# Float32r score passes on exact halves of q and k, a mask done by ScalarE and GpSimd, shared buffer pools and re-measured planner durations

## The chip, the cores and the metric

The kernel runs on one core of one Trainium2 chip. The time is the device time in microseconds of one execution; lower is better. The kernel before was timed three times: 977.66, 982.55 and 979.96 us, median 979.96 us. One execution was profiled; it took 974.69 us, of which the profile's span (first to last instruction) is 972.9 us.

The core has five engines: TensorE (PE in the profile, its weight loads PEld), VectorE (DVE), ScalarE (ACT), GpSimd (POOL) and SyncE (SP, here only a queue that issues DMAs). Each runs its own instruction list in order and waits on semaphores of the others.

## What is computed

One Macaron transformer block in float32 on x of shape (4, 1024, 256): four sequences of 1024 tokens.

```
x = x + 0.5 * ffn(layernorm(x))
x = x + attention(layernorm(x))
x = x + 0.5 * ffn(layernorm(x))

ffn(x):        hdn = silu(x @ gate_w.T * gate_s) * (x @ up_w.T * up_s)      # 704 wide, ternary weights
               out = hdn @ down_w.T * down_s
attention(x):  q, k, v = x @ Wq.T, x @ Wk.T, x @ Wv.T                       # 16 heads of 16
               q, k = rope(q), rope(k)
               out = softmax(causal(q @ k.T / 4)) @ v;  out @ Wo.T
```

## The kernel before

Tokens are worked on in 8 blocks of 512 (two blocks for each sequence). For each block there are a first FFN (`ffn(i, 1)`), `qkv(i)`, the attention, and a second FFN (`ffn(i, 2)`). The causal mask makes the second block of a sequence look at twice the keys of the first.

*FFN.* Activations and weights are in float32r, a type that TensorE multiplies in one pass where float32 takes more. An activation is kept as two float32r tiles, its rounded value and the rest (`xh` and `xnT`, `hh` and `hl`), so each product is two matmuls: L717 (gate and up, 128x512) and L804 (down, 128x256). ACT does tanh, scaling and rounding, DVE and POOL the multiplications and subtractions.

*Attention.* A group g holds 4 heads, each on 32 partitions, so that four small matmuls can stand side by side in the array ("32*128" in the profile is a matmul on 32 rows). In `qT` a head's 32 rows are 16 of q and 16 of k; DMAs (`split`, L971) copy k into the tile `kT`, whose other rows are zero but the last, which holds ones. The scores are computed twice:

- `max_half` (L1045): queries on partitions, for the maximum of each row. DVE adds the causal mask to the diagonal parts in PSUM (L1070) and takes the negated maximum (`reduce`, L1097 and L1080).
- `row_of_max` (L1119 to L1133) turns these maxima with a matmul and sends them by DMA into the last row of each head in `qT`. That row has been cleared by a DMA before (`clear`, L994).
- `exp_half` (L1158): keys on partitions. The last rows (ones against maxima) subtract the maximum within the matmul. ACT takes exp into `pT` (L1167), POOL zeroes what is masked (L1179), and `weigh` multiplies with v (L1205).

Score matmuls are float32. A "half" is two heads (a `pair`) of one unit of up to 512 columns; two halves of different pairs make a burst, so all four row groups of the array are in use. Each half takes two PSUM banks of the eight.

*The order of the work.* Nothing is ordered at run time: the class `Planner` is run while the program is built. It is a list scheduler: every operation has an engine (or a choice of DVE and POOL, `either`), a duration in us, a `tail` (time until its result can be used), the buffers it takes and a priority; bursts of scores are put in at intervals (`GAP`) between the dense matmuls. The instruction lists of all engines, and of the SP queue, come out of this plan. Each kind of tile has buffers of its own (`shapes`); `todo` is the order in which FFNs are begun. The planner's formulas for durations are `mm_us`, `dve_us` and `act_us`.

The program holds a second copy in plain float32 behind a test on the ternary weights; it is not executed here.

## Time and profile before

| what | before |
|---|---|
| three timed runs, median | 979.96 us |
| the profiled execution | 974.69 us, span 972.9 us |
| PE busy | 919.1 us (94%) |
| DVE busy | 810.8 us (83%) |
| ACT busy | 560.9 us (58%) |
| POOL busy | 542.0 us (56%) |
| granted TensorE clock, mean | 0.975 |
| DMA | 46.48 MB |

"Busy" is the union of an engine's instructions. A busy PE is not a PE at its peak, because matmuls overlap and their ends are modelled; the time from one matmul's start to the next says more. The chain of waits follows the work that ended last backwards, from each instruction to what released it. In the lists of groups, a line gives engine, operation, out<-in, shapes, count, then the busy time, the mean duration of one in ns, and the idle time of the engine before them with what ended it.

### The profile page before, as it was taken

The numbers are of one execution on the slowest core, as the hardware profiler recorded it, in microseconds if no ns is written. First come the engines' busy times: TensorE is split into PE (matmuls) and PEld (weight loads), VectorE is DVE, ScalarE is ACT, GpSimd is POOL, SyncE is SP. The second block draws the span as 40 slices with busy tenths as digits, with TensorE's granted clock in tenths as the row PEclk, the third lists the DMA queues.
The fourth block names the chain that finished last, engine by engine and source line by source line (L and its number), as shares of the span: only waits on it lengthen the run. The fifth ranks groups of instructions, "written<-read, shape, count | busy, mean of one in ns | idle before, by whom it ended". The sixth has DMA issues, their size and how long they took to land.

```text
span 972.9 us, 20459 instructions
## 1 busy us (share of the span) xinstructions
PE 919.1 (94%) x7672; PEld 525.0 (54%) x7672; DVE 810.8 (83%) x1842; ACT 560.9 (58%) x1048; POOL 542.0 (56%) x691
## 2 busy tenths in 40 slices
PE   7599998999999999998999999999999999999996
PEld 6456653465654545455556545465555453445565
DVE  5789977999798979986899978878979798997375
ACT  4554682257774555384857548268565553667663
POOL 5236785774773255755747468458652566656320
PEclk8799999999999999999999999999999998999998
DMA  8130103421302002211100302100300021020000
GB/s 295 47 85 3 44 3 76 123 66 44 88 1 88 3 14 57 67 45 39 51 1 2 110 14 77 40 8 18 92 9 16 14 73 36 26 56 7 23 23 26
DMA packets 42596, 46.48 MB, mean 48 GB/s; under 512 B 5164, under 2 KB 29996, under 8 KB 42476
## 3 DMA queue, kind: packets, MB, share of 16 engines
q1 hardware_dynamic: 41752, 44.55, 16.1%
q8 instruction: 63, 1.03, 0.4%
q10 hardware_dynamic: 736, 0.53, 0.2%
q14 instruction: 45, 0.37, 0.1%
HBM read 25.40 MB, written 15.20 MB: 42 GB/s over the span
## 4 chain that ended last, share of the span: by engine, by line
PE 66%; DVE 20%; ACT 4%; POOL 4%; issue 3%; DMA 2%; SPq 1%; ACTq 0%; DVEq 0%; POOLq 0%
PE bank L1045 14%; PE bank L717 13%; PE bank L1158 13%; PE bank L1205 11%; PE bank L804 8%; PE bank L574 7%; DVE nm L1097 5%; DVE bank L1070 2%; DVE ta L747 2%; ACT pT L1167 1%; DVE st L521 1%; DMA xnT<-xd 1%; DVE st L538 1%; DVE ta L753 1%; POOL hl L760 1%
## 5 line engine op out<-in xcount | busy, mean ns | idle before, releaser
L1167 ACT ACTIVATE pT<-bank 128x512 f32<-128x512 f32 x576 | 300.4, 602 | 186.5 <-PE bank L1158 184.3
L1097 DVE TENSOR_REDUCE nm<-bank 128x1 f32<-128x512 f32 (+2 forms) x640 | 330.8, 573 | 10.4 <-PE bank L1158 9.1
L1158 PE MATMUL bank<-qT,kT 32*128 32x512 f32 (+3 forms) x1536 | 315.8, 519 | 4.8 <-DVE ta L747 1.5
L1045 PE MATMUL bank<-kT,qT 32*128 32x512 f32 (+3 forms) x1536 | 295.9, 509 | 0.2 <-ACT tb L750 0.2
L1045 PEld LDWEIGHTS bank<-kT,qT 32*128 32x128 f32 x1536 | 128.8, 186 | 79.7 <-issue 32.8
L1158 PEld LDWEIGHTS bank<-qT,kT 32*128 32x128 f32 x1536 | 132.9, 185 | 45.8 <-issue 11.0
L1179 POOL TENSOR_SCALAR_AFFINE_SELECT pT<-pT 128x256 f32<-128x256 f32 x256 | 100.2, 413 | 96.4 <-ACT pT L1167 95.7
L717 PE MATMUL bank<-xh,wgu_sb 128*128 128x512 f32 (+1 forms) x354 | 149.9, 424 | 2.9 <-ACT xh L689 2.2
L717 PE MATMUL bank<-xnT,wgu_sb 128*128 128x512 f32 (+1 forms) x354 | 143.4, 405 | 1.5 <-POOL xnT L692 1.1
L1205 PE MATMUL bank<-pT,va 128*32 128x512 f32 (+3 forms) x1536 | 137.1, 489 | 0.8 <-ACT pT L1167 0.5
L1070 DVE TENSOR_TENSOR bank<-bank,causal 128x256 f32<-128x256 f32 (+1 forms) x320 | 103.8, 370 | 12.0 <-PE bank L1158 11.2
L753 POOL TENSOR_TENSOR ta<-ta,tb 128x512 f32<-128x512 f32 (+1 forms) x70 | 89.4, 1282 | 43.0 <-DVE ta L747 23.5
L804 PE MATMUL bank<-wd_sb,hl 128*128 128x256 f32 x320 | 87.8, 300 | 10.1 <-POOL hl L760 5.1
L717 PEld LDWEIGHTS bank<-xh,wgu_sb 128*128 128x128 f32 x354 | 68.2, 193 | 51.6 <-ACT pT L1167 20.7
L747 DVE SCALAR_TENSOR_TENSOR ta<-ta,bank 128x512 f32<-128x512 f32 (+1 forms) x96 | 64.8, 679 | 37.0 <-ACT ta L744 25.2
L760 POOL TENSOR_TENSOR hl<-ta,hh 128x512 fp32r<-128x512 f32 x63 | 81.4, 1298 | 21.3 <-ACT hh L756 19.4
L804 PE MATMUL bank<-wd_sb,hh 128*128 128x256 f32 x320 | 89.1, 305 | 4.2 <-ACT hh L756 4.2
L1205 PEld LDWEIGHTS bank<-pT,va 128*32 128x32 f32 x1536 | 44.9, 109 | 88.4 <-issue 50.0
L744 ACT ACTIVATE ta<-bank,gus_sb 128x512 f32<-128x512 f32 (+1 forms) x96 | 66.3, 691 | 35.7 <-PE bank L717 32.6
L717 PEld LDWEIGHTS bank<-xnT,wgu_sb 128*128 128x128 f32 x354 | 68.2, 193 | 17.0 <-POOL xnT L692 2.0
L804 PEld LDWEIGHTS bank<-wd_sb,hh 128*128 128x128 f32 x320 | 64.2, 201 | 22.8 <-issue 16.3
L804 PEld LDWEIGHTS bank<-wd_sb,hl 128*128 128x128 f32 x320 | 64.2, 201 | 14.1 <-POOL hl L760 7.2
(93 smaller groups left out, 1124.8 us busy)
## 6 DMA issues: line engine op xcount, KB each, us to landing
xd<-xs SPq DMA_DIRECT2D x84, 128.0 KB
xnT<-xd SPq DMA_DIRECT2D x21, 512.0 KB
rp<-in_rope SPq DMA_DIRECT2D x8, 512.0 KB
kT<-qT SPq DMA_DIRECT2D x64, 64.0 KB
out<-x SPq DMA_DIRECT2D x16, 256.0 KB
x<-in_x SPq DMA_DIRECT2D x7, 512.0 KB
qT<-nmT SPq DMA_DIRECT2D x128, 2.0 KB
tb<-in_wgu SPq DMA_DIRECT2D x5, 256.0 KB
```

Of the source, the lines that this page charges most:

```text
L717: nc.tensor.matmul(d.tile[:, j * P : (j + n) * P], wgu_sb[:, k, cols], view(t.tile[:, k])[:, j : j + n], start=k == m == 0, stop=k == NC - ...
L747: nc.vector.scalar_tensor_tensor(a.tile[up], a.tile[gate], 1.0, d.tile[gate], ALU.add, ALU.mult)
L753: e.tensor_tensor(a.tile[up], a.tile[up], u.tile[up], ALU.mult)
L760: e.tensor_tensor(hl[c].tile, a.tile, raw(hh[c].tile), ALU.subtract)
L804: nc.tensor.matmul(d.tile[:, ts(m, D)], t.tile[:, ts(j + m, P)], wd_sb[:, c, :], start=n == k == 0, stop=n == NI - 1 and k == len(halves(c ...
L1045: nc.tensor.matmul(sc[e].tile[:, c0 : c0 + w], qT[blk].tile[r, g, ts(j, P)], kt.tile[r, g, :w], start=True, stop=True,)
L1070: nc.vector.tensor_tensor(d, d, causal.unsqueeze(1).to_broadcast([P, len(masked), P]), ALU.add)
L1097: nc.vector.tensor_reduce(nm.tile[:, o : o + 1], sc[e].tile[:, c0 : c0 + w], AX.X, ALU.max, negate=True)
L1158: nc.tensor.matmul(sc[e].tile[:, c0 : c0 + w], kt.tile[r, g, ts(k % NB, P)], qT[blk].tile[r, g, BLK - w :], start=True, stop=True,)
L1167: nc.scalar.activation(pT.tile[:, e, :w], sc[e].tile[:, :w], AF.Exp)
L1179: nc.gpsimd.affine_select(out=d, in_=d, compare_op=ALU.is_ge, fill=0.0, base=0, pattern=[[0, 2], [1, P]], channel_multiplier=-1,)
L1205: nc.tensor.matmul(av.tile[ts(r, HP), BLK - w :], va[base + k // NB].tile[:, k % NB, h * VS : h * VS + HP], pTs[u, r // 2].tile[:, r % 2, ...
```

## The change

Scores (`max_half`, `exp_half`). After rope, q and k are rounded to float32r by ACT (`high`, tile `qh`) and the rest is taken by POOL or DVE (`low`, tile `ql`). DMAs build three stacks for each head's 32 rows (`moves`): `kh` holds the high half of k over its low half; `qh` holds the high half of q twice; `ql` its low half twice. One matmul of `qh` with `kh` gives (high of q) times (both halves of k), one of `ql` with `kh` the rest: two float32r passes in place of a float32 matmul. In `exp_half` a third pass, `ones` against the tile `mx`, subtracts the maximum, which itself is held in two halves. The 64 moves of k, the 16 clears and 3 loads of ones become 256 moves; the 128 sends of maxima stay, and carry two rows each.

Maxima. DVE no longer adds the mask in PSUM. It reduces the columns off the diagonal straight from PSUM; ACT copies the diagonal parts to a tile `dg` (`copy`), POOL masks them there (`affine_select`), and DVE reduces them from there. `row_of_max` joins the parts and splits the result in two halves (`halves`).

Buffers. Most SBUF kinds now share two pools, `large` (31 buffers) and `small` (22).

Planner. Tails by engine (`TAIL`), shorter durations for several operations, other costs for changes of the array's mode, bursts that emit the passes of both halves interleaved, an earlier burst where no dense matmul is at hand (`EAGER`). FFNs begin in the order of `ORDER`. Block 1's first FFN is transposed by matmuls instead of through DRAM (`TURNED`).

```diff
+ORDER = "10 11 12 13 20 14 21 15 22 16 17 23 24 25 26 27"
+PACE = 0.0
+LEAD = 20.0
+TURNED = ((0, 1), (1, 1), (7, 2))
+TAIL = dict(pe=0.25, dve=0.1, act=0.15, pool=0.1, dma=2.0)
...
+    EAGER = 0.3
-    CHANGE = dict(full=0.2, row=0.2, col=0.12)
+    CHANGE = dict(full=0.25, row=0.25, col=0.15)
...
+            if dense is None or dense > max(b[0], pe) + self.EAGER:
+                at = max(b[0], pe)
...
+                parts = []
+                for h in b[1]:
+                    t = max(at, self.pairs[h.pair])
+                    self.pairs[h.pair] = t + h.us + more
+                    parts += [(t + n * h.us / len(h.parts), f) for n, f in enumerate(h.parts)]
...
+def half_us(passes, cols):
+    return passes * cols / 2400
+
 def dve_us(n):
-    return n / 960 + 0.07
+    return n / 960 + 0.065
 def act_us(n, ptr=0):
-    return n / 1200 + 0.09 + 0.09 * ptr
+    return n / 1200 + 0.055 + 0.09 * ptr
...
+    slots = dict(large=(31, [P, 2 * BLK]), small=(22, [P, BLK]), tiny=(6, [P, D]), bank=(8, [P, BLK]))
+    shared = dict(
+        **dict.fromkeys(("x", "qh", "ql", "kh", "pT", "xnT", "xh", "xs", "rp"), "large"),
+        **dict.fromkeys(("qc", "qs", "ta", "tb", "hh", "hl", "hL", "oq", "on", "dg", "aT"), "small"),
...
-        by_dma = (i, which) not in ((0, 1), (NBLK - 1, 2))
+        by_dma = (i, which) not in TURNED
...
             def both(e=nc.gpsimd):
-                e.tensor_tensor(qT[blk].tile[:, g, :], qc.tile, qs.tile, ALU.add)
+                e.tensor_tensor(qs.tile, qc.tile, qs.tile, ALU.add)
+            def high():
+                nc.scalar.copy(qh[blk][n].tile[:, a, :], qs.tile)
+            def low(e=nc.gpsimd):
+                e.tensor_tensor(
+                    ql[blk][n].tile[:, a, :], qs.tile, qh[blk][n].tile[:, a, :].bitcast(F32), ALU.subtract
+                )
...
-        def split(gs):
+        def moves(n, which):
             def emit():
+                q, l, k = (t[blk][n].tile.bitcast(F32) for t in (qh, ql, kh))
                 for h in range(GH):
-                    nc.sync.dma_start(
-                        out=kT[blk].tile[h * HP : h * HP + HD, gs], in_=qT[blk].tile[h * HP + HD : (h + 1) * HP, gs]
-                    )
+                    lo, hi = slice(h * HP, h * HP + HD), slice(h * HP + HD, (h + 1) * HP)
+                    for to, of in ((q[hi], q[lo]), (l[hi], l[lo])) if which else ((k[lo], q[hi]), (k[hi], l[hi])):
+                        nc.sync.dma_start(out=to, in_=of)
...
+            first = Op("dma", 4.8, moves(n, 0), need, [kh[blk][n]], own, tail=2.2, prio=0)
+            T_done[1, blk, n] = Op("dma", 4.8, moves(n, 1), [first], uses=own, tail=2.2, prio=0)
...
 # max_half
+        def emit(item):
+            (g, j, _, c0, w, _), kt, n = item
+            qt = (qh, ql)[n][blk][g // 2].tile
+            for e in range(2):
+                r = ts(2 * pair + e, HP)
+                nc.tensor.matmul(
+                    sc[e].tile[:, c0 : c0 + w],
+                    qt[r, g % 2, ts(j, P)],
+                    kt.tile[r, g % 2, :w],
+                    start=n == 0,
+                    stop=n == 1,
+                )
...
-                    nc.vector.tensor_tensor(d, d, causal.unsqueeze(1).to_broadcast([P, len(masked), P]), ALU.add)
...
+                    c0, w = u[3], u[4] - P * u[5]
...
+                    nc.scalar.copy(dg.tile[:, e, : len(diag), :], of[:, diag[0] : diag[-1] + 1 : step, :])
...
+                    nc.gpsimd.affine_select(
+                        out=d,
+                        in_=d,
+                        compare_op=ALU.is_ge,
+                        fill=MASKED,
...
+                nc.vector.tensor_reduce(to, of, AX.X, ALU.max, negate=True)
...
 # row_of_max
+            nc.vector.tensor_reduce(all_, parts[:, :, 1 - blk % BPS :], AX.X, ALU.min)
...
+            nc.vector.tensor_copy(hi.bitcast(F32R), all_)
+            nc.vector.tensor_tensor(lo, all_, hi, ALU.subtract)
...
 # exp_half
+        def emit(item):
+            (g, k, c0, w), qt, n = item
+            kt = kh[base + k // NB][g // 2].tile
+            for e in range(2):
+                r = ts(2 * pair + e, HP)
+                if n < 2:
+                    key, query = kt[r, g % 2, ts(k % NB, P)], qt.tile[r, g % 2, BLK - w :]
+                else:
+                    key, query = ones[r, :], qt.tile[r, BLK - w :]
+                nc.tensor.matmul(sc[e].tile[:, c0 : c0 + w], key, query, start=n == 0, stop=n == 2)
```

## The prediction

> **What bounds the kernel now.** I read the page first: busy times, then the chain of waits; then the groups of instructions with shapes kept apart; then stretches of the timeline for what one matmul costs.
>
> ```profile
> PE 919.1 (94%) x7672; PEld 525.0 (54%) x7672; DVE 810.8 (83%) x1842; ACT 560.9 (58%) x1048; POOL 542.0 (56%) x691
> PE 66%; DVE 20%; ACT 4%; POOL 4%; issue 3%; DMA 2%; SPq 1%; ACTq 0%; DVEq 0%; POOLq 0%
> PE bank L1045 14%; PE bank L717 13%; PE bank L1158 13%; PE bank L1205 11%; PE bank L804 8%; PE bank L574 7%; DVE nm L1097 5%; DVE bank L1070 2%; DVE ta L747 2%; ACT pT L1167 1%; DVE st L521 1%; DMA xnT<-xd 1%; DVE st L538 1%; DVE ta L753 1%; POOL hl L760 1%
> ```
>
> PE is the bound, DVE close behind. The two score stages (L1045, L1158) are 27% of the span on the chain; DVE's maxima and mask (L1097, L1070) are 7%. ACT and POOL are busy nearly as long as each other and hardly on the chain. Next, starts of neighbouring matmuls in the timeline.
>
> ```profile
> 300.33 0.28 PE L804 MATMUL bank<-wd_sb,hh 128*128 128x256 f32 x1
> 300.45 0.28 PE L804 MATMUL bank<-wd_sb,hl 128*128 128x256 f32 x1
> 305.33 0.59 PE L1045 MATMUL bank<-kT,qT 32*128 32x512 f32 x2
> 305.77 0.59 PE L1045 MATMUL bank<-kT,qT 32*128 32x512 f32 x2
> 306.20 0.59 PE L1045 MATMUL bank<-kT,qT 32*128 32x512 f32 x2
> 400.26 0.40 PE L717 MATMUL bank<-xh,wgu_sb 128*128 128x512 f32 x1
> 400.50 0.40 PE L717 MATMUL bank<-xnT,wgu_sb 128*128 128x512 f32 x1
> ```
>
> Float32 scores: the next 512-column instruction of a row group starts 0.43 us after the last (305.77, 306.20), and the trace has two of them for one matmul of the program (L1045 x1536 for 768): 0.86 us. Float32r, in the FFN: one instruction, 0.24 us for 512 columns, 0.12 for 256. The groups that the change removes or cheapens:
>
> ```profile
> L1097 DVE TENSOR_REDUCE nm<-bank 128x1 f32<-128x512 f32 x384 | 240.9, 679 | 10.4 <-PE bank L1158 9.1 <-PE bank L1045 1.1
> L1070 DVE TENSOR_TENSOR bank<-bank,causal 128x256 f32<-128x256 f32 x192 | 72.5, 424 | 6.5 <-PE bank L1158 6.0 <-PE bank L1045 0.3
> L1097 DVE TENSOR_REDUCE nm<-bank 128x1 f32<-128x384 f32 x128 | 70.1, 547 | 0.0
> L1070 DVE TENSOR_TENSOR bank<-bank,causal 128x128 f32<-128x128 f32 x128 | 31.3, 291 | 5.5 <-PE bank L1158 5.2
> ```
>
> **The change part by part.** I sum against the profiled execution: span 972.9 us, 1.8 us around it; the median of the three runs is another 5.3 us longer.
>
> *Score passes, on PE.* Each stage has 384 matmuls of 512 columns and 128 each of 384, 256 and 128: 294,912 columns, over four row groups 144 steps of 512. Before: 144 x 0.86 = 124 us a stage, 248 in all. After, at 0.24 a pass: maxima 144 x 2 x 0.24 = 69, exponentials 144 x 3 x 0.24 = 104, sum 173: 75 us less. But four row groups are not always full: in a burst of one half of maxima and one of exponentials the three passes set the end, 0.72 for 0.86, and 288 such bursts save only 40 us. Taking the two instruction lists as built, and giving each matmul its time on its row group in order, without any wait, the stages come to 273 us before and 209 after. I take -64; the ends are -75 and -40. That a 32-row float32r pass takes 0.24 is no row of this trace (L717 and L804 are 128-row); it is the nearest one. The other end is the 0.43 of a 32-row float32 instruction; that is a rival below. Against weight loads: each pass still has one 128-column load per row group, of 0.19 us, under a pass of 0.24 (512 columns) but not of 0.06 (128); those are 128 of 768 and cost a few us.
>
> [...]
>
> *The mask and the maxima, on DVE.* Gone: L1070, 72.5 + 31.3 = 104 us. Reductions: before 240.9 + 70.1 + 35.9 (128 wide) + 41.0 (L1080) = 388 us; after, 256 of 512 columns at 0.627 (240.9 / 384), 128 of 384 at 0.547, 256 of 256 at about 0.41, 96 of 512 from `dg` at 0.64: 397. `halves` is three small instructions 32 times, where L1119 stood 16 times at 312 ns: +10 to +25. DVE falls from 811 to about 735 us. On the chain I credit what stands there, L1070 at 2% of the span: -20 (ends 0, where ACT's copy holds the bank as long as the mask did, and -104).
>
> *What takes its place.* ACT: 192 copies of 128x256 at 0.37 (L639, the nearest PSUM copy) and 128 of 128x128 at 0.25 (between that and L1128), 103 us; 32 roundings of q and k at 0.63, 20 us: 561 becomes 685. POOL: 128 selects of 128 columns and 96 of 512, around L1179's 413 ns for 256, at 0.25 and 0.75: 104 us; 29 of the 32 `low` at 1.3: 38 us: 542 becomes about 683. The new waits: POOL's select waits for ACT's copy, and behind it in POOL's list stand the masks of `pT` that L1205 waits for; DVE's reduction of `dg` waits for POOL, and behind it stand reductions that free PSUM banks; ACT's rounding waits for POOL's addition, and behind it stand exponentials. So 263 us of work on engines that were 58% and 56% busy. Bounds: a busy us of ACT or POOL had 0.07 us on the chain (4% for 58%), of DVE 0.24 (20% for 83%): +18 to +63. Both end near 75% busy, under DVE; I take +25.
>
> One of the new DVE instructions reads two SBUF tiles (`all_` minus `hi`). The trace shows what such a read meets beside POOL:
>
> ```profile
> L910 POOL TENSOR_TENSOR qs<-qs,rp x26: 1267/1279/1732, 57.6 to 785.1; 128x512 f32<-128x512 f32 x26
> L910 DVE TENSOR_TENSOR qs<-qs,rp x6: 681/906/1607, 55.8 to 769.9; 128x512 f32<-128x512 f32 x6
> L1119 DVE TENSOR_TENSOR nm<-nm x16: 131/166/1106, 212.8 to 888.5; 128x16 f32<-128x16 f32 x16
> ```
>
> The same instruction on DVE takes 681 to 1607 ns, and 16 columns took up to 1106. At L1119's mean of 312 ns the 32 new ones cost 10 us, which stands in the +10 to +25. [...]
>
> *Preparing q and k.* For each half block the first 4 moves become 8 (+2.4 us at 0.59 us an issue, the median of L971), the clear (0.55) becomes 8 further moves (4.7), and rounding and `low` add 1.9: 8.5 us later, 16 times, 136 us if nothing covers it. Cover: q and k of a block are made under the attention and FFNs before it. For the first block the list places 56 us of matmul time before the first maximum instead of 39. Behind these moves in SP's queue stand the FFN's trips through DRAM (L608, L614) and the sends of maxima; SP itself waits 270 us for the latter (L1133 for ACT's L1128), so it has room. I take 0; the ends are 0 and 136.
>
> *Order.* The start of block 1's first FFN:
>
> ```profile
> 43.58 0.33 PE L627 MATMUL bank<-ident,xq 128*128 128x128 f32 x1 [3.98 <-ACT xq L547]
> 46.81 0.80 PE L717 MATMUL bank<-xh,wgu_sb 128*128 128x512 f32 x1 [2.20 <-ACT xh L689]
> 48.60 0.63 PE L717 MATMUL bank<-xh,wgu_sb 128*128 128x512 f32 x1
> ```
>
> PE stands still for most of 39.6 to 46.8 while x goes through DRAM, then runs the next matmuls 0.43 us apart instead of 0.24 (the granted clock of 25 to 50 us is 0.75). With block 1 transposed by PE, between down matmuls of block 0, this gap goes: 6.2 us of idle and some 3 of slow clock, -9 (ends -12 and 0). Changes of the array's mode go from 358 to 374 in the lists, at some 0.1 us: +2. The new planner durations and the shared pools I cost at 0: 973 - 773 = 200 us of the span is not matmul time by the list (mode changes, waits, start, end), and a tenth of it, 20 us either way, is as much as I can bound.
>
> Sum: -64 - 20 + 25 - 9 + 2 = -66. Span 907, profiled execution 909, median 914 us.
>
> **The rivals.**
>
> *Larger gain.* PE and DVE both shed 8 to 9% of their work (773 to 709 by the list, 811 to 735); if the plan also removes a fifth of the 200 us, the median is 874. For it: waits of PE for single releasers are many and short. Against: ACT and POOL have less slack to give.
>
> *The gain is given back to new waits.* ACT and POOL at DVE's rate on the chain (+63 for +25) and bursts always mixed (-40 for -64): 914 + 38 + 24 = 976, no change. For it: four engines at 75 to 80%, each waiting for the others in a fixed order. Against: ACT sits idle 184 us waiting for L1158 today, so copies fit there.
>
> *Slower: float32r gains nothing in 32-row tiles.* At 0.43 us a pass, 144 x 5 x 0.43 = 310 us for 248: +62 in place of -64, median 1040. It decides from 248 / 720 = 0.344 us a pass. For it: no row shows float32r there. Against: float32 instructions of 512 columns take the same 0.43 us in 32*128 and in 128*32 tiles, so the tile shape has not mattered so far.
>
> *Slower: preparing q and k is not covered.* Beyond 66 of the 136 us the gain is gone; in full 1050. For it: both moves stand in one queue in front of other transfers. Against: L971 today ends no wait of PE that the profile names.
>
> **How the numbers follow.** Forecast, 885 to 945: 0.52. Larger gain, under 885: 0.16. Given back, 945 to 985: 0.14, of which 0.08 still faster, 0.05 within 0.5% and 0.01 slower. Float32r slow in 32-row tiles: 0.09. Preparation exposed: 0.09. So faster 0.76, same 0.05, slower 0.19; 0.5% is 4.9 us, about the spread of the three runs. The range reaches down to 862, where the larger gain leaves 0.06, and up to 1000, where 0.13 of the slower cases lie above.
>
> **What would show each step.** Right: score matmuls on one row group 0.24 us apart; PE's score lines at about 20% of the new span on the chain; DVE near 735 us, ACT near 685, POOL near 683; no gap of PE near 40 us; PE's waits for moves near zero. Wrong: passes 0.4 us apart; PE idle for DMA moves of q and k; ACT or POOL far above 8% on the chain; DVE above 780 us because its SBUF reads meet POOL more often.

## The result and the profile after

The changed kernel takes 1014.29 us (median of four, 1012.39 to 1018.04) where the kernel before took 980.16 us beside it: a ratio of 1.0353, interval 1.0314 to 1.0393. It is slower by 3.5%. The forecast was 914 us, and the time lies above its range. The profiled execution took 1018.04 us with a span of 1016.3; all sums below are of spans, 972.9 before and 1016.3 after, a difference of 43.4 us.

From the page of the changed kernel: busy times, the granted clock in 40 slices, and the chain of waits by engine and by line.

```profile
PE 928.3 (91%) x8448; PEld 576.1 (57%) x8448; DVE 769.3 (76%) x1639; ACT 653.9 (64%) x1402; POOL 666.6 (66%) x938
...
PEclk7788799969987987999988999999799898998998
...
PE 52%; DVE 21%; ACT 10%; POOL 8%; issue 4%; DMA 3%; SPq 1%; ACTq 0%; DVEq 0%; POOLq 0%
PE score L1240 12%; PE d L742 10%; PE d L1291 9%; PE d L829 7%; PE score L1073 7%; DVE nm L1102 6%; PE d L599 6%; ACT pT L1243 3%; DVE nm L1165 2%; DVE ta L772 2%; ACT dg L1134 2%; DVE oq L1327 1%; ACT ta L769 1%; ACT tb L775 1%; POOL ta L778 1%
```

The same line of the clock for the kernel before:

```profile
PEclk8799999999999999999999999999999998999998
```

Two things stand in these lines. The score lines (L1240, L1073) fell from 27% to 19% of the chain, as forecast, and PE's part from 66% to 52%; but ACT and POOL rose from 4% each to 10% and 8%. In us of the span PE lost 114 on the chain, and ACT, POOL, DVE, issue and DMA gained some 146. And the clock, which stood under 9 in 4 of the 40 slices before, does so in 17. The records of the clock show 24 stretches at half speed, 165.4 us together, where before there were 10 with 49.8 us. I call this the half clock. (The last stretch of each record runs some 2 us past the last instruction; this is so in every kernel and leaves the differences as they are.)

The passes themselves are as quick as forecast. PE's timeline of the changed kernel at full clock:

```profile
308.65 0.52 PE L1240 MATMUL score<-qh,kh 32*128 32x512 f32 x2
308.98 0.39 PE L1073 MATMUL score<-kh,ql 32*128 32x512 f32 x2
309.00 0.41 PE L1240 MATMUL score<-ql,kh 32*128 32x512 f32 x2
309.24 0.41 PE L1240 MATMUL score<-mx,ones 32*128 32x512 f32 x2
...
310.38 0.79 PE L1240 MATMUL score<-qh,kh 32*128 32x512 f32 x1 [0.48 <-ACT dg L1134]
```

309.00 to 309.24 is 0.24 us for 512 columns in a 32-row tile; over the whole trace the third pass of a half follows the second after a median of 0.234 us (335 halves at full clock). The rival of slow float32r is out. The last line shows what comes next: the following burst waits for a bank that ACT's copy still reads, and when it starts the clock is half.

### The profile page after: what moved, and what is told of

Read it like the earlier page. It is cut to its first block, busy times and chain, and to the rows that moved or that the text cites. A ratio compares the mean times of both kernels' runs of the same rounds, so it can differ in the third digit from the quotient of the medians.

```text
span 1016.3 us, 22832 instructions
## 1 busy us (share of the span) xinstructions
PE 928.3 (91%) x8448; PEld 576.1 (57%) x8448; DVE 769.3 (76%) x1639; ACT 653.9 (64%) x1402; POOL 666.6 (66%) x938
## 3 DMA queue, kind: packets, MB, share of 16 engines
q1 hardware_dynamic: 46640, 56.00, 23.5%
## 4 chain that ended last, share of the span: by engine, by line
PE 52%; DVE 21%; ACT 10%; POOL 8%; issue 4%; DMA 3%; SPq 1%; ACTq 0%; DVEq 0%; POOLq 0%
PE score L1240 12%; PE d L742 10%; PE d L1291 9%; PE d L829 7%; PE score L1073 7%; DVE nm L1102 6%; PE d L599 6%; ACT pT L1243 3%; DVE nm L1165 2%; DVE ta L772 2%; ACT dg L1134 2%; DVE oq L1327 1%; ACT ta L769 1%; ACT tb L775 1%; POOL ta L778 1%
## 5 line engine op out<-in xcount | busy, mean ns | idle before, releaser
L1243 ACT ACTIVATE pT<-score 128x512 f32<-128x512 f32 x576 | 308.4, 608 | 93.0 <-PE score L1240 91.4
L1102 DVE TENSOR_REDUCE nm<-score 128x1 f32<-128x512 f32 (+3 forms) x576 | 297.2, 562 | 62.0 <-PE score L1073 25.5
L1240 PE MATMUL score<-qh,kh 32*128 32x512 f32 (+3 forms) x768 | 216.2, 424 | 30.3 <-DVE oq L1327 9.0
L1240 PE MATMUL score<-ql,kh 32*128 32x512 f32 (+3 forms) x768 | 176.4, 377 | 0.0
L1073 PE MATMUL score<-kh,qh 32*128 32x512 f32 (+3 forms) x768 | 166.8, 402 | 8.9 <-DMA qh<-qh 3.6
L1240 PE MATMUL score<-mx,ones 32*128 32x512 f32 (+3 forms) x768 | 162.4, 358 | 0.4 <-DMA mx<-nmT 0.4
L1291 PE MATMUL d<-pT,va 128*32 128x512 f32 (+3 forms) x1536 | 154.2, 536 | 2.3 <-POOL pT L1265 2.3
L742 PE MATMUL d<-xh,wgu_sb 128*128 128x512 f32 (+1 forms) x354 | 153.8, 435 | 1.6 <-ACT xh L664 1.3
L1240 PEld LDWEIGHTS score<-qh,kh 32*128 32x128 f32 x768 | 103.9, 190 | 79.6 <-ACT pT L1243 17.2
L742 PE MATMUL d<-xnT,wgu_sb 128*128 128x512 f32 (+1 forms) x354 | 147.1, 416 | 0.0
L1073 PE MATMUL score<-kh,ql 32*128 32x512 f32 (+3 forms) x768 | 143.0, 400 | 0.0
L1073 PEld LDWEIGHTS score<-kh,qh 32*128 32x128 f32 x768 | 85.9, 195 | 69.9 <-issue 24.3
L1240 PEld LDWEIGHTS score<-mx,ones 32*128 32x128 f32 x768 | 104.1, 195 | 5.6 <-DMA mx<-nmT 1.6
L1240 PEld LDWEIGHTS score<-ql,kh 32*128 32x128 f32 x768 | 93.5, 193 | 0.1
```

What stands on the lines that cost most here:

```text
L742: nc.tensor.matmul(d.tile[:, j * P : (j + n) * P], wgu_sb[:, k, cols], view(t.tile[:, k])[:, j : j + n], start=k == m == 0, stop=k == NC - ...
L1073: nc.tensor.matmul(sc[e].tile[:, c0 : c0 + w], qt[r, g % 2, ts(j, P)], kt.tile[r, g % 2, :w], start=n == 0, stop=n == 1,)
L1102: nc.vector.tensor_reduce(nm.tile[:, o : o + step * (count - 1) + 1 : step], of, AX.X, ALU.max, negate=True)
L1240: nc.tensor.matmul(sc[e].tile[:, c0 : c0 + w], key, query, start=n == 0, stop=n == 2)
L1243: nc.scalar.activation(pT.tile[:, e, :w], sc[e].tile[:, :w], AF.Exp)
L1291: nc.tensor.matmul(av.tile[ts(r, HP), BLK - w :], va[base + k // NB].tile[:, k % NB, h * VS : h * VS + HP], pTs[u, r // 2].tile[:, r % 2, ...
```

## Where the time is: score stretches, the rest, and the clock

For each kernel I cut PE's list into score stretches (from a score matmul to the next matmul that is none) and the rest, and counted the half clock in each. All numbers are us of the profiled execution; the last column is the rest less half of its half clock, so what it would take at full clock (1 us too low throughout, for the 2 us past the span's end).

```
kernel                               span   half   score stretches   rest           rest at
                                            clock  (half clock)      (half clock)   full clock
before                               972.9   49.8  372.6  (8.9)      600.2  (40.9)   579.8
e1  before, float32r passes          978.5  132.3  358.5 (36.2)      620.0  (96.0)   572.0
e5  the same, passes alternating     977.7  125.2  358.4 (36.6)      619.4  (88.6)   575.1
e10 before, block 1 by PE            962.0   56.3  364.6 (14.7)      597.4  (41.5)   576.6
e12 before, no mask in the maxima    927.7   38.1  329.8  (0.0)      597.9  (38.1)   578.8
e13 e10 and e12 together             928.2   32.3  340.2  (3.4)      588.0  (28.9)   573.6
e14 e13 with float32r passes         913.1   63.4  313.5 (11.3)      599.6  (52.0)   573.5
e17 e14, planned with true passes    933.8  104.0  323.9 (36.9)      609.9  (67.1)   576.4
after                               1016.3  165.4  387.0 (57.4)      629.3 (108.0)   575.3
e2  after, mask on DVE              1024.9  189.0  375.6 (66.5)      649.3 (122.5)   588.0
e3  after, maxima's passes twice    1043.8  113.7  432.6 (46.8)      611.3  (67.0)   577.8
e4  after, old planner numbers      1015.3  168.3  376.9 (51.4)      638.4 (116.8)   580.0
e6  after, seven banks              1123.0  294.8  463.6 (132.4)      659.4 (162.4)   578.2
e8  after, float32 passes           1026.8   72.8  424.8 (16.8)      602.0  (56.0)   574.0
e9  after, half reductions           978.4  130.4  361.0 (42.8)      617.4  (87.7)   573.5
e11 after, no mask in the maxima     929.2   93.6  325.7 (28.4)      603.5  (65.2)   570.9
e16 after, no select                1007.6  154.1  380.8 (45.7)      626.8 (108.4)   572.6
e18 after, half of the moves        1008.9  151.5  384.8 (53.4)      624.1  (98.1)   575.1
```

In seventeen of the eighteen kernels the rest at full clock is 571 to 580 us, whatever the plan (e2, with 588, is the exception; e7 and e15 are left out, whose rest holds throwaway matmuls and long waits for transfers). Over the eighteen, the rest grows by 0.53 us (standard error 0.03) for each us of half clock in it. So the rest, which is dense matmuls, is bound by PE and costs, within some 10 us, what the clock makes of it; what the kernels differ in is the score stretches and the half clock. From before to after: the rest +29.1 us, of which the half clock is (108.0 - 40.9) / 2 = +33.6 and work -4.5; the score stretches +14.4, where the forecast had them 64 us shorter. Together 43.5.

## The experiments

All times are medians; a ratio is to the kernel before on the same chip, whose median was 976 to 978 us in these runs.

### The passes alone, the mask alone, the plan alone (e1 to e4)

e1, on the kernel before: the tiles of q and k are float32r, and each score matmul becomes passes.

```
-                    nc.tensor.matmul(sc[e].tile[:, c0 : c0 + w], qT[blk].tile[r, g, ts(j, P)], kt.tile[r, g, :w], ...)
+                    for n in range(2):            # 3 in exp_half
+                        nc.tensor.matmul(... the same, on float32r tiles ...)
```

> The kernel before, with its own order of work, mask and reductions; only the score matmuls are float32r passes, two for the maxima and three for the exponentials, on the same rounded q and k (the low halves are left out, so the scores are less exact than the reference's). Three theories of why the change was slower. Waits: the new road of the mask (ACT copies, POOL selects, DVE reduces) costs more than the passes save; then this kernel keeps the whole gain of the passes, -40 to -64 us, and takes 916 to 940 us. Clock: shorter passes leave the array less filled in the stretches that are nothing but scores, and the granted clock falls there; then most of the gain goes, the stretches at half clock grow from 50 us to 100 us or more, and the time is 960 to 990. Plan: the new planner numbers and order cost the time; then as under waits, 916 to 940, with the clock as before.

Measured: 985.19 us, ratio 1.0074 [1.0042, 1.0107]. The passes alone make the kernel a little slower. Half clock 132 us for 50, so what the clock theory expected. DVE's list is the same in both kernels, instruction for instruction; cut into 90 parts, the change in the time of a part against its change in half clock gives 0.31 us (standard error 0.02; other cuts give 0.26 to 0.31) for each us of half clock, some 25 us in all. But the parts without a change of clock got only 13 us shorter together. So the clock is one half of the answer; the other is that at full clock the passes bring little.

One pair of bursts shows how little. First PE, DVE and ACT in the kernel before, then the same instructions in e1 (both at full clock):

```profile
588.62 0.70 PE L1045 MATMUL bank<-kT,qT 32*128 32x512 f32 x2
...
589.61 0.59 PE L1045 MATMUL bank<-kT,qT 32*128 32x512 f32 x2
...
589.85 2.42 DVE L1097 TENSOR_REDUCE nm<-bank 128x1 f32<-128x512 f32 x4
589.96 2.07 ACT L1167 ACTIVATE pT<-bank 128x512 f32<-128x512 f32 x4 [0.85 <-PE bank L1158]
590.61 0.50 PE L717 MATMUL bank<-xh,wgu_sb 128*128 128x512 f32 x1
```

```profile
596.81 0.50 PE L1061 MATMUL bank<-kT,qT 32*128 32x512 f32 x2
...
597.79 0.39 PE L1061 MATMUL bank<-kT,qT 32*128 32x512 f32 x2
...
598.04 2.42 DVE L1113 TENSOR_REDUCE nm<-bank 128x1 f32<-128x512 f32 x4
598.05 2.06 ACT L1184 ACTIVATE pT<-bank 128x512 f32<-128x512 f32 x4 [0.76 <-PE bank L1175]
598.76 0.50 PE L732 MATMUL bank<-xh,wgu_sb 128*128 128x512 f32 x1
```

From the first score pass to the next dense matmul it is 1.99 us with float32 and 1.95 with float32r, though the columns need about a third less time. What ends the pair is a bank: the dense matmul starts just after ACT's first exponential has freed one (its semaphore rose at 590.56 and 598.65 us). That exponential waits for all passes of its own half, and it began 1.34 us after the pair's first pass with float32 and 1.24 us with float32r. DVE's four reductions take 2.42 us, so 1.2 for each burst, and ACT's exponentials 2.07, so 1.0; the passes of a burst need 0.86 before and 0.72 after by their columns, which is less either way. DVE's reductions do not hold up this pair, though: its second burst of maxima (589.61 and 597.79) starts before the first reduction (589.85 and 598.04).

e2, on the changed kernel: `copy` by ACT and `mask` by POOL go, DVE adds `causal` to the bank as in the kernel before.

```
-                nc.scalar.copy(dg.tile[:, e, : len(diag), :], of[:, diag[0] : diag[-1] + 1 : step, :])
-                    nc.gpsimd.affine_select(out=d, in_=d, compare_op=ALU.is_ge, fill=MASKED, ...)
+                    nc.vector.tensor_tensor(d, d, causal.unsqueeze(1).to_broadcast([P, len(masked), P]), ALU.add)
```

> The changed kernel with the mask put back on DVE, in PSUM, as before; no copies by ACT and no selects by POOL; all else is as changed, and its planner orders it anew. Waits: the 105 us that ACT and POOL gained on the chain go, DVE's 100 us of masks come back with some 30 on the chain; 930 to 960 us. Clock: the stretches of scores alone become longer by DVE's masks, the half clock stays above 130 us; 1000 to 1030. Plan: within 15 us of the changed kernel's 1014.

Measured: 1019.54 us, 1.0423 [1.0380, 1.0466]. The new road of the mask over ACT and POOL is not dearer than the old one, within the noise of the two; the theory that its waits alone cost the 35 us falls. At full clock its score stretches are 342 us (375.6 - 66.5 / 2) against 358 after, so there the road costs 16 us; that is given back in half clock and in the rest, of which this kernel has more.

e3, on the changed kernel, same plan:

```
-        items = [(u, kt, n) for u, kt in zip(unit, keys) for n in range(2)]
+        items = [(u, kt, n) for u, kt in zip(unit, keys) for n in (0, 1, 0, 1)]
```

> The changed kernel, instruction for instruction in the same order, but each of the maxima's passes is issued twice (the first two are overwritten by the same two again). That adds 288 passes' steps of 0.24 us, 69 us of matmul time. If PE's time is the bound: +40 to +69 us, 1055 to 1083. Clock: the array is better filled while DVE reduces, so the half clock falls from 165 us to under 100 and pays for most of the passes; 995 to 1030. Waits: the passes hide partly beside DVE's reductions; 1025 to 1055, with the half clock hardly changed.

Measured: 1047.16 us, 1.0725 [1.0674, 1.0776]. 69 us of passes more cost 33 us. Half clock fell from 165 to 114 us. The lists agree again: a us of half clock is worth 0.37 us here (standard error 0.03; other cuts give 0.33 to 0.38), so its fall paid back some 19 us. Several parts of the list ran faster with more work in them: the one from 305.0 to 329.2 us, with 10.2 us of half clock, took 24.2 us, and 20.5 us with the passes doubled and no half clock.

e4, on the changed kernel: `TAIL`, `CHANGE`, `EAGER`, the durations, `TURNED` and `ORDER` as before.

```
-TAIL = dict(pe=0.25, dve=0.1, act=0.15, pool=0.1, dma=2.0)
+TAIL = dict(pe=0.2, dve=0.2, act=0.2, pool=0.2, dma=2.0)
...
-TURNED = ((0, 1), (1, 1), (7, 2))
+TURNED = ((0, 1), (7, 2))
```

> The changed kernel with the planner numbers of before: tails of 0.2, mode changes of 0.2 and 0.12, the old durations of DVE, ACT and POOL, no early bursts when no dense work is at hand, block 1's first FFN by DMA and the old order of the FFNs. Plan: the loss goes, 930 to 980 us. Waits and clock: the mask's road and the short passes are still there, 1000 to 1030, though the clock theory allows 985 if bursts of scores are mixed with dense work again (half clock below 110 us).

Measured: 1016.67 us, 1.0396 [1.0354, 1.0437]. The old planner numbers do not take the loss away. They came back together with block 1's first FFN by DMA, which is worth 13.5 us in the kernel before (e10), so the new numbers by themselves may cost some 11 us: the two were not separated.

### Order within a burst, and float32 in the changed kernel (e5, e8)

e5 is e1 with PE's passes emitted in order of column time, maxima and exponentials alternating:

```
+                for _, f in sorted(parts, key=lambda x: x[0]):
+                    f()
```

> As the run of the kernel before with float32r passes (985 us): the same plan and the same matmuls, low halves left out; only PE's list differs within a burst: the passes of maxima and exponentials alternate by column time, both heads of a pair side by side, as in the changed kernel, where they stood in blocks of 4 and 6. In that run the bursts of mixed scores took as long as with float32 (their issue 196.4 us for 195.4), and an extra us of half clock cost 0.31 us. If the blocks held the passes up: bursts 40 us or more shorter, half clock some 150 us; 935 to 965 us. If the bursts are paced by weight loads, DVE and ACT: bursts within 10 us of 358; 978 to 990 us.

Measured: 983.37 us, 1.0051 [1.0024, 1.0079]; score stretches 358.4 us for 358.5. The order of the passes makes no difference in the sum, but not because nothing changed. The idle time of PE's weight loads ahead of score passes, put down to DVE and ACT, is 61 us in the kernel before, 46 in e1 and 80 in e5. So in e1, with the passes in blocks, these waits do not explain why the bursts gain so little, which points to PE's own list; in e5, with the passes alternating, the waits grew by 19 us. Before and e5 have the same 140 stretches, so they can be compared one by one, those at full clock in both sorted by the number of matmul instructions that the stretch has before. "By columns" is the stretch's matmul time spread over both pairs of row groups, at the 0.43 us of a float32 instruction and the 0.24 us of a float32r pass for 512 columns; that is a lower bound, since a burst of maxima and exponentials ends with its three passes.

```
instructions   stretches   measured, us          by columns, us
                           before    e5          before    e5
up to 8           14         16.1    11.4          12.0     7.4
9 to 20           52        106.5   100.1          79.1    55.6
21 to 32          44        116.2   111.1          78.3    55.8
33 and more       10         59.3    57.6          37.8    26.3
```

A stretch of a single burst or half of one gets the whole gain, 4.7 us of 4.6. Longer ones get 6.4 of 23.5, 5.1 of 22.5 and 1.7 of 11.5: their second burst needs banks that DVE and ACT free. That it is these banks is argued here; e6, e9 and e11 test whether the bursts of the changed kernel wait for them.

e8, the changed kernel with float32 again (one matmul of 4 steps for two passes; the exponentials keep the third pass for the maximum):

```
-        items = [(u, kt, n) for u, kt in zip(unit, keys) for n in range(2)]
+        items = [(u, kt, 0) for u, kt in zip(unit, keys)]
...
-            for n, t in enumerate((qh[blk][u[0] // 2], ql[blk][u[0] // 2], mx[blk, u[0]]))
+            for n, t in ((0, qh[blk][u[0] // 2]), (2, mx[blk, u[0]]))
```

> The changed kernel with float32 score matmuls again, one of float32 for the two passes of the maxima, and one of float32 and the float32r pass of the maximum for the exponentials; the planner counts 4 and 5 steps for 2 and 3 (the low halves of q are prepared but not used, so the scores are less exact). Preparation, mask by ACT and POOL, pools and order are as changed. If the passes lose by the clock what they gain, and the rest of the change costs the 30 us more: 1000 to 1035 us, half clock below 90 us. If the rest costs nothing and all the loss comes from the short passes and the clock: 975 to 995 us. If the passes had gained what was forecast: 1060 to 1090 us.

Measured: 1027.22 us, 1.0488 [1.0439, 1.0537]; half clock 73 us. So in the changed kernel, each planned for its own passes, the float32r passes are worth 13 us, while the half clock is 93 us more with them.

### Is the half clock a cause? (e6, e7)

The throwaway matmuls write to a PSUM bank of their own, so the control leaves the plan seven: `bank=(7, [P, BLK])`. The other kernel adds, ahead of a PE instruction that the plan starts over 0.6 us late,

```
+        if op.eng == "pe" and self.bursts and start - self.busy["pe"] > 0.6:
+            for _ in range(min(2, int((start - self.busy["pe"] - 0.4) / 0.4) + 1)):
+                self.warm()     # matmul(spare, wgu_sb[:, 0, :P], wgu_sb[:, 0, :BLK])
```

> The changed kernel with seven PSUM banks in the common pool instead of eight; planned anew. It is the control of the next run. All theories: 1000 to 1050 us, half clock 140 to 200 us.

> The control with seven banks, same plan and order, and 335 throwaway matmuls of 128x512 on all 128 rows into the eighth bank, put where the plan leaves PE idle for more than 0.6 us: 80 us of matmul time at 0.24 us, whose results nobody reads. Clock: the half clock falls by 60 us or more, and at 0.31 to 0.37 us each this is worth 19 to 30 us against what the extra matmuls delay; 0 to 30 us faster than the control. If the clock is only a sign of waits and costs nothing: no faster, 0 to 80 us slower than the control.

Measured: the control takes 1125.14 us, ratio 1.148 [1.142, 1.1539], far outside what I expected; with throwaway matmuls it takes 1098.43 us, 1.1239 [1.1170, 1.1307]. The trace has 179 of them, not the 335 of the expectation. More work made the kernel 27 us faster: the half clock fell from 295 to 191 us. So the half clock costs time by itself. And the control says something I had not asked: one bank of eight is worth 111 us. Some 65 of them go with the half clock (half of the 129 us that it grew by); of the rest, 39 lie in the score stretches, which take 397 us at full clock (463.6 - 132.4 / 2) for 358.

### What holds the banks: DVE's reductions and the mask (e9, e11, e12, e16)

e9, changed kernel, same plan, reductions over half the columns:

```
-                            reduced(column(u, e, 1 if u[2] == last else 0), 1, 1, sc[e].tile[:, c0 : c0 + w])
+                            reduced(column(u, e, 1 if u[2] == last else 0), 1, 1, sc[e].tile[:, c0 : c0 + w // 2])
```

> The changed kernel, same plan and order; each of DVE's reductions for the maxima reads the first half of its columns only (the maximum is taken over half of the keys; the other half is left out). That takes some 130 us from DVE and nothing from the other engines. If the score stretches are paced by DVE and the banks that it frees: 40 us or more off, 940 to 975 us, and less half clock because PE waits less. If PE's passes or ACT pace them: 1000 to 1014 us.

Measured: 982.54 us, 1.0037 [1.0002, 1.0072], 32 us under the changed kernel; score stretches 361.0 for 387.0, half clock 130 for 165. PE's work is untouched, so DVE holds it up; but 137 us off DVE gave 32, less than the 40 I had set for "DVE paces". ACT's share of the chain became as large as DVE's (11% each).

e11, changed kernel as in e2, but with no mask; e12, kernel before with no mask:

```
-            if masked:
+            if False:
```

> The changed kernel with no mask in the maxima at all (the masks of the exponentials stay, so masked keys still weigh nothing; a maximum may be taken over a key that is masked); planned anew. Beside the run with the mask on DVE (1019 us) it shows what DVE's mask costs, forecast 20 us; beside the changed kernel (1014) what the road over ACT and POOL costs, forecast 25 us less DVE's own reduction. If both terms are right: 985 to 1000 us. If the mask's road is beside the point, because the clock and the bursts' banks decide: 1005 to 1025 us.

> The kernel before with no mask in the maxima, planned anew; the masks of the exponentials stay. DVE loses 104 us of masks. By the prediction's term: 20 us off, 955 to 962 us. If DVE paces the score stretches: 40 us or more, below 940. If the mask lay beside other work: 972 to 980 us.

Measured: e11 933.33 us, 0.9548 [0.9486, 0.9610]; e12 930.32 us, 0.9503 [0.9456, 0.9550]. These are the largest gains of a single change in the study. In the changed kernel's plan the mask costs 86 us on DVE (e2 to e11) and 81 us on the road over ACT and POOL (after to e11); in the kernel before it costs 48. Part of the 81 is clock again: the half clock in the rest fell by 43 us, worth some 21. DVE's masks are 104 us of busy time in the kernel before, on the chain with 2%.

e16, changed kernel, same plan, the body of POOL's `mask` left out:

```
-                    nc.gpsimd.affine_select(out=d, in_=d, compare_op=ALU.is_ge, fill=MASKED, ...)
+                pass
```

> The changed kernel, same plan and order, without POOL's selects in the mask of the maxima: ACT copies the diagonal squares and DVE reduces them unmasked (so a maximum may be taken over a masked key; the masks of the exponentials stay). POOL loses some 95 us. If the wait for POOL in the mask's road makes it dear: 970 to 990 us. If the copy by ACT and the two reductions, which hold the banks, make it dear: within 12 us of 1014.

Measured: 1008.79 us, 1.0327 [1.0283, 1.0372]. POOL's part of the road is at most some 5 us, within the noise of the two. What is left is ACT's copy and DVE's reductions. Their groups in the changed kernel (busy, mean ns, idle time before and what ended it):

```profile
L1102 DVE TENSOR_REDUCE nm<-score 128x1 f32<-128x384 f32 x128 | 67.0, 551 | 20.9 <-ACT dg L1134 11.6 <-PE score L1073 6.6 <-PE score L1240 1.7
L1134 ACT COPY dg<-score 128x256 f32<-128x256 f32 x192 | 65.7, 390 | 51.5 <-DVE nm L1102 29.2 <-PE score L1073 11.6 <-DVE nm L1165 5.8
L1165 DVE TENSOR_REDUCE nm<-dg 128x4 f32<-128x512 f32 x96 | 63.7, 675 | 21.2 <-POOL dg L1145 21.1
L1145 POOL TENSOR_SCALAR_AFFINE_SELECT dg<-dg 128x512 f32<-128x512 f32 x96 | 60.3, 637 | 37.5 <-ACT dg L1134 37.1
```

ACT's copy waits for DVE's reduction and DVE's reduction for ACT's copy: both read the same bank of scores, and one stands behind the other, so a bank with a diagonal is held for both times where these waits stand. In the kernel before it was held for the mask and the reduction. Whether it is this or the longer way to the maximum that costs the 81 us was not separated.

### The other terms of the forecast (e10, e15, e18)

e10, the kernel before with block 1 transposed by PE:

```
-        by_dma = (i, which) not in ((0, 1), (NBLK - 1, 2))
+        by_dma = (i, which) not in ((0, 1), (1, 1), (NBLK - 1, 2))
```

> The kernel before, with block 1's first FFN transposed by PE instead of through DRAM and nothing else of the change; planned anew. The prediction gave this 9 us. If right: 965 to 972 us, no gap near 40 us. If the gap only moves, or a new plan costs more than it is worth: 976 to 990 us.

Measured: 964.64 us, 0.9859 [0.9810, 0.9909], 13.5 us off. Right, and rather more than the 9 us.

e15 and e18 bracket the moves of q and k: each issued twice, and half of them left out.

```
+                        for _ in range(2):                                                             # e15
                             nc.sync.dma_start(out=to, in_=of)
...
-                    for to, of in ((q[hi], q[lo]), (l[hi], l[lo])) if which else ((k[lo], q[hi]), (k[hi], l[hi])):
+                    for to, of in () if which else ((k[lo], q[hi]), (k[hi], l[hi])):                   # e18
```

> The changed kernel, same plan and order; each of the 256 moves of q's and k's halves is issued twice (the second writes the same again), so SP's queue carries 256 more issues of some 0.6 us before the waits that follow them. If preparing q and k is on the path: 30 us or more slower, above 1044 us. If it is covered, as the prediction had it: within 8 us of 1014.

> The changed kernel, same plan and order, without the second half of the moves that prepare q and k (128 of 256): k's halves are moved, q's halves are not copied to the upper rows, where k's halves stay, so each score has a small term of k with itself in place of q's product with k's low half. SP issues 128 moves fewer (76 us) and the scores may start some 5 to 7 us earlier in each of the 16 half blocks. If preparing q and k is covered, as the prediction had it: within 8 us of 1014. If it is on the path: 30 us or more faster, below 985.

Measured: e15 1497.64 us, 1.5327 [1.5258, 1.5396]; e18 1011.76 us, 1.0348 [1.0310, 1.0386]. e15 loaded far more than I meant, as SP's waits there show:

```profile
SPq L1014 <- DMA kh<-qh: 117.0, 64, 4.2
SPq L1014 <- DMA qh<-qh: 115.3, 64, 3.5
```

The second copy of each move waited for the first to land, 456 us over the four kinds, besides 256 issues at 0.6 us; the sends of the maxima stood behind them, and PE waited for those. So e15 does not measure the moves. e18 does: with 128 moves fewer the kernel is 2.5 us faster, and the intervals overlap. Preparing q and k is covered.

### Passes without a mask, and a faster kernel (e13, e14, e17)

e13 joins e10 and e12; e14 is e13 with e5's passes, same plan; e17 is e14 planned anew with 2 and 3 steps (`mm_us(...) / 2` and `0.75 * mm_us(w)`).

> The kernel before with two changes that gained alone: no mask in the maxima (930 us alone) and block 1's first FFN transposed by PE (965 alone); scores in float32. It is the control of the next run. If the two gains add: 912 to 922 us. If they overlap: 925 to 935.

> The control without mask, same plan and order, with float32r passes on rounded q and k (low halves left out), alternating as the changed kernel's do. Banks: the passes gained nothing because DVE's masks and reductions held the PSUM banks; without the mask PE is the bound, so they gain 64 us less the clock's share, 30 us or more below the control. Loads and order within the burst: the passes can't run at 0.24 us in mixed bursts whatever DVE does; within 12 us of the control, with half clock 50 us or more above it.

> The kernel of 920 us (before, block 1 transposed by PE, no mask in the maxima, float32r passes on rounded q and k), planned anew with the true steps of the passes, 2 and 3 for 4 and 4. If the freed time on PE is to be had by a plan that knows of it: 880 to 905 us. If the bursts are paced by ACT and DVE, 1.2 us each for 512 columns, and by the clock: 910 to 930 us.

Measured: e13 932.39 us, 0.9556 [0.9512, 0.9599], so the two gains don't add; e14 920.00 us, 0.9433 [0.9383, 0.9483]; e17 933.97 us, 0.9525 [0.9474, 0.9577]. The chain of waits in e13 and then in e14:

```profile
PE 78%; DVE 12%; ACT 3%; POOL 3%; issue 2%; DMA 1%; ACTq 0%; SPq 0%; DVEq 0%; POOLq 0%
```

```profile
PE 63%; DVE 17%; ACT 7%; POOL 5%; DMA 4%; issue 2%; SPq 1%; ACTq 0%; DVEq 0%; POOLq 0%
```

With PE on 78% of the chain, the passes bring 12 us; with the mask they had cost 5 (before to e5). It is still below the 30 of the banks theory. At full clock the score stretches get 31 us shorter (338.5 to 307.8), about what they got with the mask (368.2 to 340.1, 28 us). So the mask is not what keeps the passes from their 64 us, and the clock takes some 12 us back in the rest. The pace of DVE's reductions and ACT's exponentials, 1.2 and 1.0 us a burst, is still there, and so are PE's own order and weight loads; which of them keeps the rest of the gain no run separates. e17 has score stretches and rest at full clock as in e14 (305 and 576 us for 308 and 574); its 20.7 us of longer span (14 us by the medians) are the half clock, (104.0 - 63.4) / 2 = 20.3. A plan that knows of the shorter passes packs the same work and loses by the clock. e14 beats both kernels, with scores on rounded q and k and a shift of the softmax that may come from a masked key; the changed kernel's low halves would have to be added to it.

## Why the prediction was wrong, by its own steps

- *Score passes, -64.* This step failed. Its price of a pass was right (0.24 us). The step from there to the path was not: "the three passes set the end, 0.72 for 0.86" left out what other engines do for the same burst: DVE's reductions take 1.2 us for 512 columns, with the masks 1.7 on average (388 + 104 us over 288 halves), and ACT's exponentials 1.0. The rows were at hand (679 and 424 ns in the prediction, 602 on the page before), but I compared them only as sums over the span, DVE's 735 against PE. Measured at full clock: -28 in the score stretches (e5) and -31 without the mask (e14), below the end of -40 that I had put to it; alone, and with the clock, +5. That the bursts of the changed kernel wait for DVE is shown by e9. How the missing 36 us divide between DVE, ACT and PE's own list is not: the waits for DVE and ACT account for 19 of them in e5.
- *No term for the clock.* The forecast's sum had 3 us of slow clock, at the start. From before to after the half clock grew by 116 us and cost 33.6 us in the rest; in the score stretches up to another 24. It is the largest single item of the 43 us from before to after. The line of the clock was in the page, and so was a drop that I read as idleness.
- *DVE's mask, -20, and the new waits, +25.* The net was nearly right (+5 forecast, -5 measured from e2 to after, which is within the noise), and that was luck, for both sizes were wrong by a factor of 3 to 4 in the changed kernel's plan: -86 and +81 (in the kernel before the mask is worth 48). The forecast's +25 also priced 263 us of new work on ACT and POOL, which by its own figures are 265. The share of the chain for each busy us (0.24 for DVE, 0.07 for ACT and POOL) is no price for an instruction that holds a bank which the next burst needs.
- *Busy times.* ACT 654 us and POOL 667 for the forecast 685 and 683; DVE 769 for 735. The reductions cost 387 us as forecast (397); the surplus is `halves` (26.5 us for three lines, above my 10 to 25) and DVE's share of work on two SBUF tiles: the addition that makes q and k rose from 7.6 us (7 at 1082 ns) to 16.3 (12 at 1360 ns). Seven of the 12 took 1.65 to 1.77 us, and each of these began while a POOL TENSOR_TENSOR was running and ended 0.55 us after it. The small subtraction had a median of 176 ns, for the 166 of L1119.
- *Preparing q and k, 0.* Right (e18).
- *Block 1's first FFN, -9.* Right in the kernel before (-13.5, e10). Planner and pools at 0 within 20 us: e4 has +2 for the planner's numbers and block 1 together; the pools were not tried. Mode changes were not measured by themselves.
- *The rivals.* "Given back to new waits" named the engines that took the chain over, at 976 us, but as a price of ACT's and POOL's extra work; e8 shows the loss with float32 passes too, and e16 that POOL's part is 5 us. Slow float32r and exposed preparation are refuted. None of the rivals had the clock.

At full clock throughout (half of all half clock taken off), the sum reads: passes -28 in the score stretches (e5), the mask's new road +16 there (e2 to after), the rest -5; -17 in all, where before to after has 948.0 to 933.6, -14. The half clock adds 58 by the same count, of which 34 are certain, since the score stretches may not have needed the clock.

## What to carry to other kernels

Price a faster matmul by the burst and not by the sum: put beside its passes what each other engine does for the same banks, and take the gain only where PE is the longest of them or where one burst stands alone. Look at the granted clock after every shortened matmul: here the half clock grew by 116 us from before to after, which cost some 34 us in dense matmuls that were not touched. Don't price an instruction that holds a bank between two bursts by its share of the chain: DVE's mask had 2% of it, some 20 us, and was worth 48 in the kernel before, where the passes gave 28 in the score stretches at full clock (e5).

## What the runs showed of the hardware

The clock halved while PE was busy. Windows of the changed kernel (from and to, length, busy us of PE, PEld, DVE, ACT and POOL with instructions, granted clock, DMA):

```profile
371.70:375.10 3.40, 3.06 (x39) 2.20 (x37) 3.28 (x8) 2.66 (x6) 2.56 (x5) 1.00 0.51 82
375.10:385.30 10.20, 9.89 (x73) 5.45 (x75) 5.75 (x14) 5.70 (x15) 4.49 (x13) 0.50 0.12 21
...
716.40:719.80 3.40, 2.63 (x30) 1.61 (x28) 1.75 (x4) 2.58 (x7) 3.08 (x4) 1.00 0.68 140
719.80:730.00 10.20, 10.20 (x55) 5.23 (x54) 6.25 (x14) 6.31 (x14) 5.66 (x9) 0.50 0.18 53
```

From 371.7 to 375.1 PE has matmuls in flight for 3.06 of 3.40 us, and then runs at half the clock for 10.2 us; ahead of the drop at 719.8 it is 2.63 of 3.40. The changed kernel's 24 stretches of half clock lasted 3.4 to 17.1 us. Where the passes of the scores became shorter the half clock grew: 132 us for 50 from before to e1, 63 for 32 from e13 to e14. Where they became longer, or were issued twice, it fell: 73 us in e8 and 114 in e3, for 165 in the changed kernel. With half reductions or no mask it fell too, to 130 us in e9 and 94 in e11, and with 179 throwaway matmuls of 128x512 on all 128 rows from 295 to 191 us (e6 to e7). My reading, that bursts of short passes which other engines pace bring the clock down, fits all of these; what it is in a burst that does so, no run shows.

The half clock outlasts the scores: 108 of the 165 us lay in the rest, on dense matmuls. There the starts of neighbouring 128x512 matmuls stand 427 ns apart (median) for 233 at full clock, those of 128x256 ones 214 for 116. And the number of PSUM banks mattered more than the mask: in the changed kernel seven for eight cost 111 us, the mask 81 to 86.
